# A two-layer block with test-time training, experts and latent attention: attention's weight folds cut into pieces behind single heads, their transposes made by loads and VectorE, and the values' bias as weighted sums

## The chip, the cores and the metric

The kernel runs on one core of a Trainium2 chip. The metric is the device time of one execution in microseconds. TensorE is called PE below, VectorE DVE, ScalarE ACT, GpSimd POOL; SP (SyncE) issues most of the transfers.

## The reference

The model is two residual blocks in float32 over x of shape [4, 512, 512]. Block one adds a test-time-training attention (a scan of 32 mini-batches of 16 tokens, which updates a small weight matrix per head in each step) and a gated feed-forward of width 1408. Block two adds a latent attention (16 heads of 128 over 512 tokens, as four sequences) and four experts, where token t goes to expert t mod 4. The change concerns block two's attention and the last lines of block one:

```python
c_kv = hidden_states @ W_DKV + b_DKV
k = (c_kv @ W_UK + b_UK).reshape(b, s, H, D)
v = (c_kv @ W_UV + b_UV).reshape(b, s, H, D)
c_q = hidden_states @ W_DQ + b_DQ
q = (c_q @ W_UQ + b_UQ).reshape(b, s, H, D)
...
q_r = q @ W_QR
k_r = k @ W_KR
...
q = q.at[..., :RD].set(rope(q_r))
k = k.at[..., :RD].set(rope(k_r))
scores = jnp.einsum('bqhd,bkhd->bhqk', q, k) / jnp.sqrt(jnp.float32(D))
probs = jax.nn.softmax(scores, axis=-1)
ctx = jnp.einsum('bhqk,bkhd->bqhd', probs, v).reshape(b, s, H * D)
return ctx @ W_O + b_O
```

H is 16, D 128, RD 64. c_kv has 128 columns and c_q 384 (three tiles of 128).

## The kernel before, in words

**Folded weights.** The kernel multiplies weights with weights so as to save work per token. Per head, W_UK W_KR and W_UQ W_QR (128 to 64 columns) take the place of the rotated half of keys and queries, and W_UV W_O (128x512, called vo) lets the latents themselves be the values. Each product contracts over D, so the weight must be turned first. `group_weights(hg)` does that for a group of four heads: it loads uk, uq0 to uq2, uv and W_O's rows ow (L948, L962); five times it turns a block's four 128x128 squares on PE against the identity (ptw, L937) and copies the result out of PSUM with ACT (wt, L939); four of the blocks are multiplied by W_KR or W_QR (pw, L955; copied by ACT, L956), the fifth by ow, four times (pvo, L970; copied, L971). The values' bias b_UV becomes a constant row through W_O, since a softmax row sums to 1: b_O + W_O^T b_UV, the tile bo. `value_bias(hg)` computes it during the first stage: 16 loads of W_O rows (wob), 16 matmuls with b_UV spread over 32 columns, and for each group a matmul with ones (1/32) and an add.

**Stage 1, the scan** (0 to about 946 us). The 32 steps run in sequence; 4 steps are a chunk, 8 chunks (NCHUNK) the whole. Between the parts of a step stands other PE work, the filler: next chunk's keys and queries, feed-forward tiles, the norm and output projection of finished chunks (`finish`), `value_bias`, and the second block's latents. This order is written out by hand: every generator yields the PE time of its piece in microseconds, and `fill(us)` takes pieces until that much is used. START, three GAPS per step, LAST_GAPS for the last chunk and LAST_FINISH for the pieces of the last `finish` set how much. A scheduler then orders each engine's queue.

**The tail of stage 1** (946 to 1022 us): the last chunk's z goes through DRAM to zb, is normed twice and projected (L546 to L601). `latents(key)` multiplies the normed rows by W_DKV and W_DQ; each of four 128-column results m is copied out by ACT with its bias, one quarter per sequence (L637), into a tile lat of two buffers and stored to DRAM (lat_d, L640, on ACT's queue). POOL's queue meanwhile loads the experts' gate weights and the rows xe (14 of 16; the last two on SP, L831).

**Stage 2, the experts** (1022 to 1191 us): for each of four experts, four pairs of gate and up products (epg, epu, L855), SiLU on ACT, a product on DVE (inter), then four down products (epo, L900), added to y by DVE (L907), and y += bo by POOL (L908). All PSUM tiles come from one pool d_ps.

**Stage 3, attention** (1191 to 2161 us): 64 units (4 groups of heads, 4 sequences, 4 heads). Per unit: keys and queries (pk L992, pq L999) with the rotation by DVE (L978, L982) and an add on POOL (L985); scores (sc L1008), row maximum (mx L1010, DVE), exponentials and their scaling (L1013, L1015, ACT); DVE turns 32x32 blocks (tt, L1023); 16 transfers per unit, all on SP, put the blocks in place (prT<-tt, L1046); three units later the context (pc L1054), and per four units the output projection (po L1069). `group_weights` of the next group stands ahead of the unit where sequence 1 begins; group 0's ahead of the first unit.

Of the kernel before, what the change touches and what calls it, by code (L numbers as in the profile page):

```python
# [12 lines left out]
F32 = mybir.dt.float32  # L13
AF = mybir.ActivationFunctionType
# [21 lines left out]
START = 20.0  # L36
GAPS, LAST_GAPS = (11.0, 4.0, 8.0), (10.0, 4.0, 5.0)
LAST_FINISH = (9.0, 17.0, 5.0)
TTT_EPS = 1e-6
# [16 lines left out]
def trunk_kernel(ctx: ExitStack, tc: tile.TileContext, a: dict, out: bass.AP):  # L56
# [32 lines left out]
    with ExitStack() as px:  # L89
# [423 lines left out]


        ones32 = one.tile([P, P], F32, tag="ones32", name="ones32")
        nc.vector.memset(ones32, 1.0 / 32)
        buv16 = one.tile([H, D], F32, tag="buv16", name="buv16")
        nc.gpsimd.dma_start(out=buv16, in_=a["b_UV"].rearrange("(h d) -> h d", d=D))
        buv_b = one.tile([P, H, 32], F32, tag="buv_b", name="buv_b")
        nc.gpsimd.dma_start(out=bo, in_=a["b_O"].unsqueeze(0).to_broadcast([P, HS]))  # L520

        def value_bias(hg):
            if hg == 0:
                pt = psum()[:, :H]
                nc.tensor.transpose(pt, buv16, ident[:H, :H])
                nc.vector.tensor_copy(buv_b, pt.unsqueeze(2).to_broadcast([P, H, 32]))
            pb = psum()
            for h, r in enumerate(quarters):
                w = wk.tile([P, HS], F32, tag="wd", name=f"wob_{hg}_{h}", bufs=4)
                nc.sync.dma_start(out=w, in_=a["W_O"][(4 * hg + h) * D : (4 * hg + h + 1) * D, :])  # L530
                mm(pb[r], buv_b[:, 4 * hg + h, :], w)
            part = wk.tile([P, HS], F32, tag="xt", name=f"bo_part{hg}", bufs=4)
            nc.vector.tensor_copy(part, pb)
            yield 1.3
            pb = psum()
            mm(pb, ones32, part)
            nc.vector.tensor_add(bo, pb, bo)
            yield 0.86

        def over_blocks(t, z):  # L540
# [83 lines left out]
        def latents(key):  # L624
# [4 lines left out]
            for m, w in enumerate(lw):  # L629
                pl = psum()[:, : n * CW]  # L630
                for c in range(NC):
                    mm(pl, w[:, c, :], part[:, :, c], c == 0, c == NC - 1)
                st = wk.tile([P, 512], F32, tag="xs", name=f"lat_{ks[0]}_{m}")
                view = pl.rearrange("p (k u e b j) -> p k u e b j", k=n, u=2, e=E, b=2)
                to = st[:, : n * CW].rearrange("p (b k e j) -> p b k e j", b=B, k=n, e=E)
                for b in range(B):
                    nc.scalar.activation(  # L637
                        to[:, b], view[:, :, b // 2, :, b % 2], AF.Identity, bias=lat_b[:, m : m + 1], scale=1.0
                    )
# [6 lines left out]
        nc.gpsimd.dma_start(out=lat_b[:, :1], in_=a["b_DKV"])  # L646
        nc.gpsimd.dma_start(out=lat_b[:, 1:], in_=a["b_DQ"])


        def between(ch):  # L650
# [10 lines left out]
            if ch == 0:  # L661
                yield from finish_constants()
            extra = value_bias(ch - 1) if 1 <= ch <= NHG else iter(())
            nxt = iter(())
# [12 lines left out]
            yield from extra  # L677
            yield from nxt
# [116 lines left out]
        for us in LAST_FINISH:  # L795
            fill(us)
            next(fin)
        for _ in chain(work, fin, latents(NCHUNK - 1)):
            pass
# [19 lines left out]
    lv = lat.tile([P, B, E, KVC], F32, tag="lv", name="lv")  # L819

    with ExitStack() as px:
        one = px.enter_context(tc.tile_pool(name="d_one", bufs=1, reuse_waits="tile"))
        wk = px.enter_context(tc.tile_pool(name="d_wk", bufs=2, reuse_waits="tile"))
        wg = px.enter_context(tc.tile_pool(name="d_wg", bufs=1, reuse_waits="tile"))
        psp = px.enter_context(tc.tile_pool(name="d_ps", bufs=2, space=PSUM))
        gate_w = [one.tile([P, NC, 2 * EI], F32, tag="gu1", name="gu_1")]
        gate_w.insert(0, wg.tile([P, NC, 2 * EI], F32, tag="gu0", name="gu_0"))
# [41 lines left out]
        for e in range(E):  # L869
# [3 lines left out]
            if e == 1:  # L873
                nc.sync.dma_start(out=wqr, in_=a["W_QR"])
                nc.sync.dma_start(out=wkr, in_=a["W_KR"])
                nc.sync.dma_start(out=buk, in_=a["b_UK"])
                nc.sync.dma_start(out=buq, in_=a["b_UQ"])
# [9 lines left out]
            for i in range(EI // P):  # L887
                pg = psp.tile([P, B * P], F32, tag="pg", name=f"epg_{e}_{i}")
                product(e, pg, gu, i * P)
                pu = psp.tile([P, B * P], F32, tag="pu", name=f"epu_{e}_{i}")  # L890
                product(e, pu, gu, EI + i * P)
# [5 lines left out]
            for b in range(B):  # L897
# [9 lines left out]
                nc.vector.tensor_add(y[b][:, e, :], po, y[b][:, e, :])  # L907
                nc.gpsimd.tensor_add(y[b][:, e, :], y[b][:, e, :], bo)  # L908
            if e == 1:

                for wr, bias in ((wkr, buk), (wqr, buq)):
                    pb = psp.tile([P, 512], F32, tag="pa", name="pb")
                    nc.tensor.matmul(pb[RD:, :H], lhsT=wr, rhs=bias, start=True, stop=True)
                    nc.vector.tensor_copy(bias[RD:, :], pb[RD:, :H])
                nc.vector.tensor_scalar_mul(buq[:RD, :], buq[:RD, :], scale)
                nc.vector.tensor_scalar_mul(trig_q[RD:, :], trig_k[RD:, :], scale)
# [11 lines left out]
    with ExitStack() as px:  # L928
        wk = px.enter_context(tc.tile_pool(name="e_wk", bufs=2, reuse_waits="tile"))
        ps_pj = px.enter_context(tc.tile_pool(name="e_pspj", bufs=4, space=PSUM))  # L930
        ps_sc = px.enter_context(tc.tile_pool(name="e_pssc", bufs=4, space=PSUM))

        def turned(w, nm):

            pt = ps_pj.tile([P, HPG, P], F32, tag="pj", name=f"ptw_{nm}")
            for h in range(HPG):
                nc.tensor.transpose(pt[:, h, :], w[:, h, :], ident)  # L937
            t = wk.tile([P, HPG, P], F32, tag="wt", name=f"wt_{nm}")
            nc.scalar.copy(t, pt)  # L939
            return t  # L940

        def group_weights(hg):

            c = slice(hg * HPG * D, (hg + 1) * HPG * D)

            def loaded(name, src, bufs=2):
                t = wk.tile([P, HPG, src.shape[-1] // HPG], F32, tag=name, name=f"{name}_{hg}", bufs=bufs)
                nc.sync.dma_start(out=t, in_=src.rearrange("p (h d) -> p h d", h=HPG))  # L948
                return t

            def fold(w, wr, nm):
                wt = turned(w, f"{nm}_{hg}")
                pw = ps_pj.tile([P, HPG, RD], F32, tag="pj", name=f"pw_{nm}_{hg}")
                for h in range(HPG):
                    nc.tensor.matmul(pw[:, h, :], lhsT=wt[:, h, :], rhs=wr, start=True, stop=True)  # L955
                nc.scalar.copy(w[:, :, RD:], pw)  # L956

            uk = loaded("uk", a["W_UK"][:, c])
            uq = [loaded(f"uq{i}", a["W_UQ"][i * P : (i + 1) * P, c]) for i in range(QC // P)]
            uv = loaded("uv", a["W_UV"][:, c], bufs=1)  # L960
            ow = wk.tile([P, HPG, HS], F32, tag="ow", name=f"ow_{hg}", bufs=1)
            nc.sync.dma_start(out=ow, in_=a["W_O"][c, :].rearrange("(h p) o -> p h o", p=P))  # L962
            fold(uk, wkr, "uk")
            for i in range(QC // P):
                fold(uq[i], wqr, f"uq{i}")
            uvt = turned(uv, f"uv_{hg}")
            vo = wk.tile([P, HPG, HS], F32, tag="vo", name=f"vo_{hg}")
            for h in range(HPG):
                pv = ps_pj.tile([P, HS], F32, tag="pj", name=f"pvo_{hg}_{h}")
                nc.tensor.matmul(pv, lhsT=uvt[:, h, :], rhs=ow[:, h, :], start=True, stop=True)  # L970
                nc.scalar.copy(vo[:, h, :], pv)  # L971
            return dict(uk=uk, uq=uq, vo=vo)

# [13 lines left out]
        def queries_keys(hg, b, h, w):  # L987
# [10 lines left out]
            for i in range(nq):  # L998
                nc.tensor.matmul(  # L999
                    pq, lhsT=w["uq"][i][:, h, :], rhs=cq[:, i, b, :], start=(i == 0), stop=(i == nq - 1)  # L1000
                )
# [208 lines left out]
```

## Time and profile before

| | us |
|---|---|
| three runs, median | 2162.95 |
| three runs, lowest and highest | 2159.44, 2164.58 |
| the profiled execution | 2162.4 |
| its span in the trace | 2160.6 |
| mean granted PE clock | 0.987 |

The profile's page gives the busy time of each engine, the span in 40 equal slices, the transfers, the chain of work that ended last, and the costliest groups of instructions. These are its slices for PE and its clock, in tenths, and for the transfers' rate:

```profile
PE   8999999999999999995999899999999999999998
...
PEclk9999999999999999998999989999999999999999
DMA  6556364646474646526610233333233333333332
GB/s 179 153 138 190 112 193 134 180 135 175 131 197 129 173 136 192 171 75 235 226 59 25 89 92 77 74 94 75 76 77 93 75 72 78 75 75 75 95 94 76
```

One digit covers 54 us; a 9 stands for 90% or more. The 5 is the tail of stage 1. By groups, in PE, the largest of stage 3 and the transfers that belong to it:

```profile
L1008 PE MATMUL sc<-kT,qT 96*128 96x512 f32 x512 | 235.7, 598 | 15.1 <-ACT prob L1013 13.5
...
L1023 DVE STREAM_TRANSPOSE tt<-prob 128x512 f32<-128x512 f32 x252 | 166.6, 697 | 60.3 <-ACT prob L1015 56.7
...
prT<-tt SPq DMA_DIRECT2D x1008, 64.0 KB, 2.0
```

A group's row gives line, engine, operation, output and inputs, the shape and the number of instructions; then busy time and the mean of one in ns; then the idle time of the engine just before, and what ended most of it. The last row gives KB of one transfer and the median time from issue to landing. A matmul of float32 shows as two records.

### The profile page before, as it was taken

The numbers are of one execution on the slowest core, as the hardware profiler recorded it, in microseconds if no ns is written. First come the engines' busy times: TensorE is split into PE (matmuls) and PEld (weight loads), VectorE is DVE, ScalarE is ACT, GpSimd is POOL, SyncE is SP. The second block draws the span as 40 slices with busy tenths as digits, with TensorE's granted clock in tenths as the row PEclk, the third lists the DMA queues.
The fourth block names the chain that finished last, engine by engine and source line by source line (L and its number), as shares of the span: only waits on it lengthen the run. The fifth ranks groups of instructions, "written<-read, shape, count | busy, mean of one in ns | idle before, by whom it ended". The sixth has DMA issues, their size and how long they took to land.

```text
span 2160.6 us, 29279 instructions
## 1 busy us (share of the span) xinstructions
PE 2068.6 (96%) x10050; PEld 1181.5 (55%) x10050; DVE 1177.5 (54%) x2384; ACT 883.3 (41%) x1805; POOL 504.9 (23%) x555
## 2 busy tenths in 40 slices
PE   8999999999999999995999899999999999999998
PEld 6776676767676767543444444444444444444444
DVE  4445656465656565631111556664666656666663
ACT  2334353434434343332000454444544545455552
POOL 4233233233333333301001211110111111111110
PEclk9999999999999999998999989999999999999999
DMA  6556364646474646526610233333233333333332
GB/s 179 153 138 190 112 193 134 180 135 175 131 197 129 173 136 192 171 75 235 226 59 25 89 92 77 74 94 75 76 77 93 75 72 78 75 75 75 95 94 76
DMA packets 286960, 259.27 MB, mean 120 GB/s; under 512 B 52956, under 2 KB 210845, under 8 KB 285789
## 3 DMA queue, kind: packets, MB, share of 16 engines
q1 hardware_dynamic: 272752, 245.96, 41.0%
q10 hardware_dynamic: 11500, 5.32, 0.9%
q0 software_dynamic: 2560, 6.13, 0.8%
q8 instruction: 81, 1.33, 0.3%
q14 instruction: 67, 0.54, 0.1%
HBM read 161.60 MB, written 29.62 MB: 89 GB/s over the span
## 4 chain that ended last, share of the span: by engine, by line
PE 75%; DVE 10%; ACT 9%; DMA 3%; issue 2%; POOL 1%; SPq 0%; ACTq 0%; DVEq 0%; POOLq 0%
PE pj L100 14%; PE pf L100 11%; PE po L1069 10%; PE pc L1054 7%; PE sc L1008 5%; PE pq L999 5%; PE pd L100 5%; ACT prob L1013 3%; PE epg L855 3%; PE epo L900 3%; PE epu L855 3%; ACT prob L1015 2%; PE pso L100 2%; PE pk L992 2%; PE pz L100 2%
## 5 line engine op out<-in xcount | busy, mean ns | idle before, releaser
L1008 PE MATMUL sc<-kT,qT 96*128 96x512 f32 x512 | 235.7, 598 | 15.1 <-ACT prob L1013 13.5
L985 POOL TENSOR_TENSOR kT<-t_k,t_k 32x512 f32<-32x512 f32 x64 | 80.7, 1261 | 717.9 <-PE pq L999 403.3
L1013 ACT ACTIVATE prob<-sc,mx 128x512 f32<-128x512 f32 x256 | 173.1, 683 | 147.1 <-DVE mx L1010 147.1
L1069 PE MATMUL po<-vo,ctxT 128*128 128x512 f32 x512 | 223.0, 593 | 1.5 <-ACT ctxT L1059 1.5
L1054 PE MATMUL pc<-prT,lv 128*128 128x512 f32 x496 | 224.0, 594 | 0.0
L1023 DVE STREAM_TRANSPOSE tt<-prob 128x512 f32<-128x512 f32 x252 | 166.6, 697 | 60.3 <-ACT prob L1015 56.7
L100 PE MATMUL pf<-xT,wg 128*128 128x256 f32 x704 | 171.8, 385 | 4.2 <-DVE hid L459 3.9
L999 PE MATMUL pq<-cq,uq 128*128 128x512 f32 x384 | 175.2, 592 | 0.0
L1015 ACT ACTIVATE prob<-prob,sm 128x512 f32<-128x512 f32 x256 | 171.7, 724 | 3.6 <-DVE sm L1014 3.6
L1008 PEld LDWEIGHTS sc<-kT,qT 96*128 96x128 f32 x512 | 96.0, 191 | 140.9 <-issue 110.6
L100 PE MATMUL pf<-xT,wu 128*128 128x256 f32 x704 | 168.0, 380 | 0.5 <-DMA wu<-in_wu 0.3
L1010 DVE TENSOR_REDUCE mx<-sc 128x1 f32<-128x512 f32 x256 | 164.4, 681 | 7.0 <-PE sc L1008 4.4
L100 PE MATMUL pd<-wd,hid 128*128 128x512 f32 x352 | 165.2, 600 | 0.2
L1069 PEld LDWEIGHTS po<-vo,ctxT 128*128 128x128 f32 x512 | 97.1, 190 | 124.1 <-issue 116.2
L1054 PEld LDWEIGHTS pc<-prT,lv 128*128 128x128 f32 x496 | 94.5, 191 | 120.0 <-issue 112.1
L100 PEld LDWEIGHTS pf<-xT,wg 128*128 128x128 f32 x704 | 131.0, 190 | 32.1 <-DVE hid L459 6.7
L100 PEld LDWEIGHTS pf<-xT,wu 128*128 128x128 f32 x704 | 133.2, 190 | 22.1 <-issue 2.6
L1079 DVE TENSOR_TENSOR y<-po,y 128x512 f32<-128x512 f32 x64 | 44.2, 691 | 152.5 <-PE po L1069 152.5
L993 ACT ACTIVATE kT<-pk,b_UK 64x512 f32<-64x512 f32 x64 | 43.7, 683 | 196.7 <-PE pk L992 196.7
L999 PEld LDWEIGHTS pq<-cq,uq 128*128 128x128 f32 x384 | 73.0, 190 | 91.8 <-issue 86.8
L459 DVE SCALAR_TENSOR_TENSOR hid<-pf,us,sg 128x256 f32<-128x256 f32 x88 | 41.5, 474 | 132.6 <-ACT sg L458 132.0
L297 POOL TENSOR_SCALAR sk<-k,m 128x256 f32<-128x256 f32 x64 | 61.3, 969 | 158.1 <-PE pz L100 158.1
(256 smaller groups left out, 3151.8 us busy)
## 6 DMA issues: line engine op xcount, KB each, us to landing
prT<-tt SPq DMA_DIRECT2D x1008, 64.0 KB, 2.0
wd<-in_wd SPq DMA_DIRECT2D x176, 256.0 KB, 3.0
wg<-in_wg SPq DMA_DIRECT2D x88, 256.0 KB, 3.5
wu<-in_wu SPq DMA_DIRECT2D x88, 256.0 KB, 3.4
rows<-rows SPq DMA_DIRECT2D x128, 66.0 KB, 2.2
kv<-rows SPq DMA_DIRECT2D x32, 264.0 KB, 4.4
gu<-in_gu SPq DMA_DIRECT2D x3, 2048.0 KB, 8.7
xt<-in_x SPq DMA_DIRECT2D x32, 128.0 KB, 3.2
```

Of the source, the lines that this page charges most:

```text
L100: nc.tensor.matmul(out, lhsT=lhsT, rhs=rhs, start=start, stop=stop, skip_group_check=True)
L855: nc.tensor.matmul(ps, lhsT=w[:, c, col : col + P], rhs=xe[:, :, c, e, :], start=(c == 0), stop=(c == NC - 1))
L900: nc.tensor.matmul(po, lhsT=inter[:, i, b * P : (b + 1) * P], rhs=dn[:, i, :], start=(i == 0), stop=(i == EI // P - 1),)
L985: nc.gpsimd.tensor_sub(t[RD:mid, :], t1[RD:mid, :], t2[RD:mid, :])
L999: nc.tensor.matmul(pq, lhsT=w["uq"][i][:, h, :], rhs=cq[:, i, b, :], start=(i == 0), stop=(i == nq - 1))
L1008: nc.tensor.matmul(ps, lhsT=qT[:KQ, i * P : (i + 1) * P], rhs=kT[:KQ, :], start=True, stop=True)
L1010: nc.vector.tensor_reduce(mx, ps, AX.X, ALU.max, negate=True)
L1013: nc.scalar.activation(pr, ps, AF.Exp, bias=mx, scale=1.0, accum_out=sm)
L1015: nc.scalar.mul(pr, pr, sm)
L1023: nc.vector.transpose(out=tt[:, :, :, i, :], in_=pr.rearrange("p (kb e j) -> p kb e j", e=2, j=K))
L1054: ins = nc.tensor.matmul(pc, lhsT=lv[:, b, k, :], rhs=prT[:, k, :], start=(k == 0), stop=(k == E - 1))
L1069: ins = nc.tensor.matmul(po[e], lhsT=ctxT[:, h, e * P : (e + 1) * P], rhs=w["vo"][:, h, :], start=(h == 0), stop=(h == HPG - 1),)
```

## The change

Its parts:

- The filler's budgets: the middle gap of a step is 3 for 4, in the last chunk (10, 3, 7) for (10, 4, 5); LAST_FINISH has six entries, and after them come the last latents, then the rest of the filler.
- `value_bias` is gone from stage 1. Each fold multiplies its heads' ow rows by b_UV (one scalar per row) on DVE into a running sum bo_part; after the last group one matmul with ones sums over rows and adds to bo. POOL's y += bo goes from the experts to the last 16 units of attention.
- `latents`: odd m are copied out by DVE, even m by ACT.
- In the experts, gate and up tiles have a PSUM pool of their own, ps_gu.
- `fold` takes the place of `group_weights`. For uk and uq only the RD columns that stay are loaded into the weight tile. The block to be turned comes as 16 loads of 32 partitions with four runs of 128 bytes each (raw), which put the 32x32 squares where the transpose wants them; DVE's stream transpose turns the squares (wt). ow is loaded by heads. `fold` yields between pieces: block i is loaded, block i-1 turned, block i-2 multiplied.
- Group 0's fold runs in pieces among experts 1 to 3, with one buffer each for raw and wt; the others' advance by a piece behind each unit whose head isn't the first of a sequence, with two buffers each.

```diff
-GAPS, LAST_GAPS = (11.0, 4.0, 8.0), (10.0, 4.0, 5.0)
-LAST_FINISH = (9.0, 17.0, 5.0)
+GAPS, LAST_GAPS = (11.0, 3.0, 8.0), (10.0, 3.0, 7.0)
+LAST_FINISH = (10.0, 14.0, 7.0, 0.0, 3.0, 1.0)
...
-        def value_bias(hg):
...
-            for h, r in enumerate(quarters):
-                w = wk.tile([P, HS], F32, tag="wd", name=f"wob_{hg}_{h}", bufs=4)
-                nc.sync.dma_start(out=w, in_=a["W_O"][(4 * hg + h) * D : (4 * hg + h + 1) * D, :])
-                mm(pb[r], buv_b[:, 4 * hg + h, :], w)
...
                 for b in range(B):
...
+                    part_b = view[:, :, b // 2, :, b % 2]
+                    if m % 2:
+                        nc.vector.tensor_scalar(to[:, b], part_b, lat_b[:, m : m + 1], None, ALU.add)
+                    else:
+                        nc.scalar.activation(to[:, b], part_b, AF.Identity, bias=lat_b[:, m : m + 1], scale=1.0)
...
-        for _ in chain(work, fin, latents(NCHUNK - 1)):
+        for _ in chain(latents(NCHUNK - 1), work):
             pass
...
+    def fold(w, hg, wk, psum, bufs):
...
+        for nm, src in zip(ups, srcs):
+            nc.sync.dma_start(out=w[nm][:, :, :RD], in_=src.rearrange("p (h d) -> p h d", h=HPG)[:, :, :RD])
...
+        def output_rows(h):
+            ows[h] = wk.tile([P, HS], F32, tag="ow", name=f"ow_{hg}_{h}", bufs=2)
+            nc.sync.dma_start(out=ows[h], in_=a["W_O"][(hg * HPG + h) * D : (hg * HPG + h + 1) * D, :])
...
+        for i in range(n + 2):
+            if 0 <= i - 2 < n - 1:
+                wt, wr, to = turned.pop(i - 2), wkr if i == 2 else wqr, w[ups[i - 2]]
+                pw = psum(f"pw_{hg}_{i}").rearrange("p (h d) -> p h d", h=HPG)[:, :, :RD]
+                for h in range(HPG):
+                    nc.tensor.matmul(pw[:, h, :], lhsT=wt[:, h, :], rhs=wr, start=True, stop=True)
+                nc.scalar.copy(to[:, :, RD:], pw)
+            if 0 <= i - 1 < n:
+                t = turned[i - 1] = wk.tile([P, HPG, P], F32, tag="wt", name=f"wt_{hg}_{i - 1}", bufs=bufs)
+                nc.vector.transpose(
+                    out=t.rearrange("p h c -> p (h c)"), in_=raws.pop(i - 1).rearrange("p h c -> p (h c)")
+                )
+            if i < n:
+
+                raw = raws[i] = wk.tile([P, HPG, P], F32, tag="raw", name=f"raw_{hg}_{i}", bufs=bufs)
+                view = srcs[i].rearrange("(cq r) (h dq d) -> dq r h cq d", r=32, h=HPG, dq=4)
+                for dq, r in enumerate(quarters):
+                    for h in range(HPG):
+                        nc.sync.dma_start(
+                            out=raw[r, h].rearrange("r (cq d) -> r cq d", cq=4), in_=view[dq, :, h]
+                        )
+            if i >= n:
+                output_rows(i - n)
+            yield
+        wt = turned.pop(n - 1)
+        for h in range(HPG):
+            pv = psum(f"pvo_{hg}_{h}")
+            nc.tensor.matmul(pv, lhsT=wt[:, h, :], rhs=ows[h], start=True, stop=True)
+            nc.scalar.copy(w["vo"][:, h, :], pv)
+            hh = hg * HPG + h
+            if hh == 0:
+                nc.vector.tensor_scalar_mul(bo_part, ows[h], buv[:, :1])
+            else:
+                nc.vector.scalar_tensor_tensor(bo_part, ows[h], buv[:, hh : hh + 1], bo_part, ALU.mult, ALU.add)
+            if h + 2 < HPG:
+                output_rows(h + 2)
+            if h == 1:
+                yield
+        if hg == NHG - 1:
+            pb = psum("pbo")
+            nc.tensor.matmul(pb, lhsT=ones, rhs=bo_part, start=True, stop=True)
+            nc.vector.tensor_add(bo, pb, bo)
...
+        ps_gu = px.enter_context(tc.tile_pool(name="d_psgu", bufs=2, space=PSUM))
...
+                first = fold(w0, 0, wk, lambda nm: psp.tile([P, 512], F32, tag="pa", name=nm), 1)
...
             for i in range(EI // P):
-                pg = psp.tile([P, B * P], F32, tag="pg", name=f"epg_{e}_{i}")
+                if e > 1:
+                    next(first, None)
+                pg = ps_gu.tile([P, B * P], F32, tag="pg", name=f"epg_{e}_{i}")
...
-                nc.gpsimd.tensor_add(y[b][:, e, :], y[b][:, e, :], bo)
+            if e in (1, 2):
+                next(first, None)
...
-        ws[0] = group_weights(0)
+        folds = iter(())
+        ws[0] = w0
...
-                        ws[hg + 1] = group_weights(hg + 1)
+                        ws[hg + 1] = group_tiles((lat, wk)[(hg + 1) % 2], hg + 1)
+                        folds = fold(
+                            ws[hg + 1], hg + 1, wk, lambda nm: ps_pj.tile([P, 512], F32, tag="pj", name=nm), 2
+                        )
...
+            if i % HPG != 0:
+                next(folds, None)
+            if 0 <= i - len(units) + HPG * B < HPG * B:
+                b, e = divmod(i - len(units) + HPG * B, HPG)
+                nc.gpsimd.tensor_add(y[b][:, e, :], y[b][:, e, :], bo)
```

More of the change, by code (lines that the diff above doesn't have):

```diff
@@ L512, in finish_constants @@
             yield 3.43
[L515 to L520, printed above, removed]
-        def value_bias(hg):
[L523 to L527, printed above, removed]
-            for h, r in enumerate(quarters):
-                w = wk.tile([P, HS], F32, tag="wd", name=f"wob_{hg}_{h}", bufs=4)
-                nc.sync.dma_start(out=w, in_=a["W_O"][(4 * hg + h) * D : (4 * hg + h + 1) * D, :])
-                mm(pb[r], buv_b[:, 4 * hg + h, :], w)
[L532 to L538, printed above, removed]
         def over_blocks(t, z):
@@ L636, in latents @@
                 for b in range(B):
-                    nc.scalar.activation(
-                        to[:, b], view[:, :, b // 2, :, b % 2], AF.Identity, bias=lat_b[:, m : m + 1], scale=1.0
-                    )
+                    part_b = view[:, :, b // 2, :, b % 2]
[3 more added lines that the diff above has]
+                        nc.scalar.activation(to[:, b], part_b, AF.Identity, bias=lat_b[:, m : m + 1], scale=1.0)
                 nc.scalar.dma_start(
@@ L646, in trunk_kernel @@
         nc.gpsimd.dma_start(out=lat_b[:, :1], in_=a["b_DKV"])
+        nc.gpsimd.dma_start(out=bo, in_=a["b_O"].unsqueeze(0).to_broadcast([P, HS]))
         nc.gpsimd.dma_start(out=lat_b[:, 1:], in_=a["b_DQ"])
@@ L662, in between @@
                 yield from finish_constants()
-            extra = value_bias(ch - 1) if 1 <= ch <= NHG else iter(())
             nxt = iter(())
@@ L676, in between @@
                     yield from take(fin, 1)
-            yield from extra
             yield from nxt
@@ L819, in trunk_kernel, with group_tiles @@
     lv = lat.tile([P, B, E, KVC], F32, tag="lv", name="lv")
+    quarters = [slice(32 * q, 32 * q + 32) for q in range(4)]
+    buv = lat.tile([P, H], F32, tag="b_UV", name="b_UV")
+    bo_part = lat.tile([P, HS], F32, tag="bo_part", name="bo_part")
+    ones = lat.tile([P, P], F32, tag="ones", name="ones")
+    nc.gpsimd.memset(ones, 1.0)
+    ups = ["uk"] + [f"uq{i}" for i in range(QC // P)]
+    def group_tiles(pool, hg):
+        w = {nm: pool.tile([P, HPG, D], F32, tag=nm, name=f"{nm}_{hg}", bufs=1) for nm in ups}
+        w["vo"] = pool.tile([P, HPG, HS], F32, tag="vo", name=f"vo_{hg}", bufs=1)
+        return w
@@ new lines, in fold @@
+    def fold(w, hg, wk, psum, bufs):
+        c = slice(hg * HPG * D, (hg + 1) * HPG * D)
+        srcs = [a["W_UK"][:, c]] + [a["W_UQ"][i * P : (i + 1) * P, c] for i in range(QC // P)]
+        for nm, src in zip(ups, srcs):
+            nc.sync.dma_start(out=w[nm][:, :, :RD], in_=src.rearrange("p (h d) -> p h d", h=HPG)[:, :, :RD])
+        srcs.append(a["W_UV"][:, c])
+        raws, turned, ows = {}, {}, {}
+        def output_rows(h):
+            ows[h] = wk.tile([P, HS], F32, tag="ow", name=f"ow_{hg}_{h}", bufs=2)
+            nc.sync.dma_start(out=ows[h], in_=a["W_O"][(hg * HPG + h) * D : (hg * HPG + h + 1) * D, :])
+        n = len(srcs)
+        for i in range(n + 2):
[39 more added lines that the diff above has]
+            nc.vector.tensor_add(bo, pb, bo)
@@ L875, in trunk_kernel @@
                 nc.sync.dma_start(out=wkr, in_=a["W_KR"])
+                buv16 = wk.tile([H, D], F32, tag="buv16", name="buv16", bufs=1)
+                nc.sync.dma_start(out=buv16, in_=a["b_UV"].rearrange("(h d) -> h d", d=D))
+                w0 = group_tiles(lat, 0)
+                first = fold(w0, 0, wk, lambda nm: psp.tile([P, 512], F32, tag="pa", name=nm), 1)
                 nc.sync.dma_start(out=buk, in_=a["b_UK"])
@@ L887, in trunk_kernel @@
             for i in range(EI // P):
-                pg = psp.tile([P, B * P], F32, tag="pg", name=f"epg_{e}_{i}")
+                if e > 1:
+                    next(first, None)
+                pg = ps_gu.tile([P, B * P], F32, tag="pg", name=f"epg_{e}_{i}")
                 product(e, pg, gu, i * P)
-                pu = psp.tile([P, B * P], F32, tag="pu", name=f"epu_{e}_{i}")
+                pu = ps_gu.tile([P, B * P], F32, tag="pu", name=f"epu_{e}_{i}")
                 product(e, pu, gu, EI + i * P)
@@ L914, in trunk_kernel @@
                     nc.vector.tensor_copy(bias[RD:, :], pb[RD:, :H])
+                pb = psp.tile([P, 512], F32, tag="pa", name="pbuv")
+                nc.tensor.transpose(pb[:, :H], buv16, ident[:H, :H])
+                nc.vector.tensor_copy(buv, pb[:, :H])
                 nc.vector.tensor_scalar_mul(buq[:RD, :], buq[:RD, :], scale)
@@ L931, in trunk_kernel @@
         ps_sc = px.enter_context(tc.tile_pool(name="e_pssc", bufs=4, space=PSUM))
[L933 to L972, printed above, removed]
         def rotate(t, ps, bias, trig, nm):
@@ L999, in queries_keys @@
                 nc.tensor.matmul(
-                    pq, lhsT=w["uq"][i][:, h, :], rhs=cq[:, i, b, :], start=(i == 0), stop=(i == nq - 1)
+                    pq, lhsT=w[f"uq{i}"][:, h, :], rhs=cq[:, i, b, :], start=(i == 0), stop=(i == nq - 1)
                 )
```

## The prediction

> **What bounds the kernel now.** I read the page first: busy time by engine, then the chain of work that ended last.
>
> ```profile
> PE 2068.6 (96%) x10050; PEld 1181.5 (55%) x10050; DVE 1177.5 (54%) x2384; ACT 883.3 (41%) x1805; POOL 504.9 (23%) x555
> ...
> PE 75%; DVE 10%; ACT 9%; DMA 3%; issue 2%; POOL 1%; SPq 0%; ACTq 0%; DVEq 0%; POOLq 0%
> ```
>
> TensorE is the bound: only 92 us of the 2160.6 us span are idle on it. So a gain is either a matmul taken away or one of these idle stretches closed. Next, windows by stage show where they lie. In the scan:
>
> ```profile
> 54.00:400.00 346.00, 334.06 (x2609) 241.76 (x2608) 190.39 (x443) 138.14 (x250) 106.89 (x134) 0.99 0.53 151
> 400.00:900.00 500.00, 488.81 (x3925) 355.82 (x3924) 299.22 (x668) 204.83 (x376) 170.95 (x205) 1.00 0.57 164
> ```
>
> The second number is the window's length, the third PE busy: 97 to 98%, so PE work removed here is time removed. Between scan and experts it is otherwise:
>
> ```profile
> 963.13:981.26 18.13, 16.46 (x52) 9.66 (x53) 9.21 (x6) 8.27 (x26) 5.92 (x8) 1.00 0.25 70
> 981.26:993.57 12.31, 0.60 (x3) 0.22 (x2) 2.34 (x3) 1.98 (x5) 4.68 (x9) 0.69 1.04 404
> 993.57:1008.48 14.91, 11.57 (x28) 5.62 (x29) 4.84 (x11) 2.02 (x5) 0.00 (x0) 0.80 0.34 102
> 1008.48:1022.40 13.92, 7.18 (x33) 6.00 (x33) 0.00 (x0) 3.71 (x16) 0.00 (x0) 0.91 0.82 255
> ```
>
> From the scan's end at 946.25 to the first expert matmul at 1022.40 are 76.15 us with 49.81 busy: 26.3 idle, at a clock down to 0.69. The timelines of PE and ACT tell what ends the waits:
>
> ```profile
> 993.57 0.98 PE L100 MATMUL pj<-onesd,pn_sq 128*128 128x1 f32 x4 [11.71 <-DVE pn_sq L543]
> ...
> 1022.40 2.07 PE L855 MATMUL epg<-xe,gu 128*128 128x512 f32 x2 [6.74 <-ACT lat L637]
> ```
> ```profile
> 989.66 0.93 ACT L637 ACTIVATE lat<-pj,lat_b 128x64 f32<-128x64 f32 x4 [8.70 <-DMA lat_d<-lat]
> ...
> 1019.84 0.93 ACT L637 ACTIVATE lat<-pj,lat_b 128x64 f32<-128x64 f32 x4 [6.67 <-DMA lat_d<-lat]
> ```
>
> A bracket is the idle time before the row and its releaser. Twice ACT stands 7 to 9 us for the store of a latent tile two tiles back, under loads of 404 GB/s. The first hold keeps up the last chunk's norm, the second the first expert matmul, which waits for PSUM that ACT frees. The experts (1022.4 to 1191.3) are all PE: 168.90 busy of 168.90. Then the first fold stands alone:
>
> ```profile
> 1192.75 0.63 PE L937 MATMUL ptw_uk<-ident,uk 128*128 128x128 f32 x4 [0.83 <-issue]
> ...
> 1204.43 5.31 PE L970 MATMUL pvo<-ow,wt_uv 128*128 128x512 f32 x8 [0.73 <-ACT wt_uv L939]
> 1209.58 0.59 PE L992 MATMUL pk<-ckv,uk 128*128 128x512 f32 x1
> ```
>
> Three rows price the rest:
>
> ```profile
> L100 PE MATMUL pj<-wob,buv_b x32: 592/593/1057, 262.5 to 611.0; 128*32 128x512 f32 x32
> L277 SPq DMA_DIRECT2D rows<-rows x128: 303/430/1938, 31.2 to 827.5; - x128
> L1046 SPq DMA_DIRECT2D prT<-tt x1008: 585/599/1982, 1227.7 to 2137.0; - x168
> ```
>
> **The change, part by part** (against the profiled execution: 2162.4 us, span 2160.6; the median of the runs, 2162.95, is 0.5 above).
>
> 1. *value_bias out of the scan.* 16 wob matmuls of two records; a pair steps by about 0.98 us, so 15.7; four ones matmuls at 0.86 (a pair like pk's, 1.02 with its overlap), 3.4; one transpose 0.15. **−19**: PE has 2 to 3% idle there, so it all counts, unless the gaps' smaller fill (middle gap 4 to 3) uncovers the scan's serial chain; then −10. Its replacement, 16 DVE weighted sums of 0.75 us, lies among experts and attention, where the windows show DVE 14 and 62 to 67% busy: nothing; uncovered 12.
>
> 2. *Tail.* With pg and pu in PSUM of their own, the first expert matmul waits for DMAs only: the 6.7 us go, and about 2 us of half-clock records behind them. Half the latent evacuations go to DVE and one chunk's latents (13.7 us of PE work) are left for the end: they fill idle time. But ACT's and DVE's order of the changed kernel still has latent tiles, each waiting for a store two tiles back, between the steps of the last norm, and xe's last two stores behind them on ACT. So I don't credit the 8.7 us hold; it may move to another step of the norm. Ends: −2 (a new hold eats it) and −24 (nearly all idle gone). Taken: 6.7 + 2 + 3 of filled idle: **−12**.
>
> 3. *Group 0's fold among the experts.* Added to a stage with no idle PE: four pw of 0.84 (1491.80 to the next start at 1492.64 in group 2), four pvo matmuls in 3.5, pbuv 0.15: +7. wt_3 on DVE stands ahead of inter_3 and waits for 16 raw loads: behind it epo's operand and PE; bounded by 0 and one burst (7), taken +1; the cold fold start goes, −2. **+6**. The 18.1 us from 1191.3 to pk at 1209.4 go: **−18**. What is late next is pk's operands cq and ckv, loaded by then in both.
>
> 4. *Folds 1 to 3.* 15 blocks of four PE transposes at 0.44 (start to next start, 1489.63 to 1490.08), 6.6 us. The waits for wt copies are 0.7 + 8.4 + 2.8 = 11.9 in all groups (waits by releaser), less 3.6 in group 0: 8.3. Now wt comes from DVE a unit (10 us) before PE wants it. **−15**. DVE gets 20 stream transposes of 0.70 (tt's row): hidden; each waits for 16 loads, with mx and tt queued behind, and sc and prT behind those; a burst plus landing is 6.9 + 2, under the 10 us of a unit.
>
> 5. *320 raw loads on SP*, the unknown. SP issues 16 prT per unit, 10.3 us of a PE unit of 10.3 (13.7 with po); the order has 48 of a group's 80 raw loads between units 22 and 26 (likewise 6 to 10, 38 to 42). From the first prT of 22 (1567.5) to the last that 26's context (1637.7) allows are 58 us with landing; four units' prT take 41. So the stall per group is 48c − 17, where c is the issue of one raw load. Ends: 0.30 (the rows' minimum) gives none, with 1 at unit 23, whose slack is 4.6; 0.60 (prT) gives 12; 0.43 gives 4. A raw load reads DRAM in 128 runs, as rows' loads move 128 runs; prT goes SBUF to SBUF. I take 0.43: 3 × 4 = **+12**, with +3 and +36 as ends. The 12 further ow loads (about 0.4 each, 5 us) follow unit 26, where SP stands idle for DVE's tt (239 us in all); uk and uq stay four issues per group.
>
> Here the Trainium skill speaks against the change: "DMA: Bandwidth & Descriptors", Bandwidth, says transfers under 64 KB are descriptor-dominated and lists 0.68 us of engine time for 4 KB, 0.95 for 64 KB. A raw load is 16 KB in 128 B runs; interpolated between these, an estimate of 0.75 us each would make the stall 19 per group, 57 in all, and the whole time 2165: no gain. In this trace prT, itself 64 KB, lands after 2.0 us yet one is issued each 0.6: three or more are under way at once. So I take the issue, not the transfer.
>
> 6. *y += bo on POOL in the last 16 units*, 1.26 each. Nine stand back to back before group 3's first kT and qT: 11 us that rotations wait behind, and sc behind them; one to two units of lead cover most. With pbo 0.9: **+3** (1 to 12).
>
> Sum: −19 − 12 + 6 − 18 − 15 + 12 + 3 = −43; 2162.4 − 43 = 2119.4, with the 0.5 of the median **2120**.
>
> **Rivals.**
>
> - *Raw loads at prT's 0.60*: part 5 becomes 36, 2144 (2135 to 2158). For it: the same 32 partitions and four runs on each; against: rows and kv at 0.43. 18%.
> - *Slower: SP becomes the bound in the attention.* The other parts sum to −55; they are eaten from 48c − 17 = 18.4 on, c = 0.74. At c = 1.0, as trig's four strided loads show in the median (1.02, lanes waited for), 31 per group, 93 in all: 2201. SP's queue is in order, so prT, the contexts and DVE's tt all stand behind a burst. Against: trig's loads meet the 2 MB expert loads. 9%.
> - *Scan and tail give nothing back*: gaps too short (−10) and the latents hold the last norm (−2): +19, 2139. For it: ACT's order; against: the PSUM wait goes in any case. 12%.
> - *More than forecast*: raw loads at 0.30 (+3) and the tail −24: 2099. 13%.
>
> My forecast (2106 to 2135) has 48%. The range holds forecast, cheap and dear raw loads and the lost tail: **2092 to 2154**. A measurement can't tell under 0.2% (4.3 us) from no change. Faster 0.88, same 0.03, slower 0.09.
>
> **What would show it.** SP's row for raw: 0.43, and prT of units 7, 10, 23, 26, 39, 42 waiting on nothing but the queue, with pc there idle 2 to 5 us. Experts about 176 us long, their first matmul without ACT as releaser, within 70 us of the scan's end. No gap after the last epo. Scan 19 us shorter. In all, PE busy falls by about 27 us (19, and 9 of 80 transposes, less pbuv and pbo) and its idle by about 16. I am wrong if raw issues take 0.6 or more, if DVE waits for raw loads while sc waits for mx, or if ACT still stands on latent stores during the last norm.

## The result: slower by 2.7%, and the profile after

| | us |
|---|---|
| before, median of 4 runs | 2163.76 |
| the changed kernel, median of 4 runs | 2222.43 (2216.11 to 2222.76) |
| ratio, 95% interval | 1.0267 (1.0243 to 1.0291) |
| its profiled execution: span | 2220.5 |

The forecast was 2120. On the page of the changed kernel, TensorE is busy for longer than before although it executes 118 instructions less, and the scores' row has another releaser:

```profile
PE 2074.2 (93%) x9932; PEld 1177.6 (53%) x9932; DVE 1204.0 (54%) x2452; ACT 851.6 (38%) x1733; POOL 505.2 (23%) x555
...
L1025 PE MATMUL sc<-kT,qT 96*128 96x512 f32 x512 | 261.5, 652 | 55.2 <-POOL qT L1002 37.4
```

Before, this group took 235.7 us at 598 ns each, behind 15.1 us of idle time. A mean of 652 ns means that part of the scores ran slower; the timelines below show them at half clock. Windows by stage say where the time is. First before, from the scan to the end; then the changed kernel, cut at the same events (last matmul of the scan, first epg, first pk). The third number is PE busy; the granted clock stands behind POOL's busy time:

```profile
0.00:946.30 946.30, 913.98 (x7197) 655.80 (x7197) 540.92 (x1240) 370.98 (x699) 312.78 (x395) 0.99 0.55 157
946.30:1022.40 76.10, 49.76 (x150) 27.45 (x147) 16.98 (x22) 22.18 (x72) 10.60 (x16) 0.89 0.56 178
1022.40:1209.60 187.20, 182.79 (x465) 84.62 (x466) 23.89 (x36) 19.15 (x33) 20.22 (x16) 0.97 0.31 110
1209.60:2160.60 951.00, 922.08 (x2245) 413.59 (x2243) 595.70 (x1086) 470.94 (x1003) 161.25 (x128) 0.99 0.32 81
```
```profile
0.00:928.40 928.40, 888.33 (x7124) 647.48 (x7124) 538.57 (x1233) 350.68 (x668) 313.41 (x394) 0.99 0.54 154
928.40:1035.50 107.10, 65.22 (x179) 33.99 (x178) 25.94 (x61) 16.79 (x49) 10.75 (x17) 0.82 0.54 180
1035.50:1214.00 178.50, 177.60 (x446) 80.96 (x446) 29.47 (x46) 16.92 (x29) 0.00 (x0) 0.98 0.31 90
1214.00:2220.50 1006.50, 943.06 (x2186) 415.17 (x2186) 610.02 (x1114) 467.25 (x987) 181.00 (x144) 0.96 0.33 78
```

Scan −17.9, tail +31.0, experts with the first fold −8.7, attention +55.5: together +59.9, the difference of the spans. The scan gained about what was forecast (−19), and the experts with the first fold a part of it (+6 − 18 = −12); the tail and the attention went the other way. In the attention PE has 59 instructions less and 21 us more busy time, and 63 us of idle time where it had 29. The list of PE's waits (total, times, longest) has the largest of each at its head:

```profile
PE sc L1025 <- POOL qT L1002: 37.4, 12, 5.9
PE epg L903 <- DMA xe<-xe_d: 33.6, 1, 33.6
```

**The tail.** The first expert matmul no longer waits for ACT, as forecast; it waits for the rows xe. POOL's timeline shows why they are late:

```profile
964.34 0.83 POOL L892 DMA_DIRECT2D gu<-in_gu  x1
1005.79 4.26 POOL L896 DMA_DIRECT2D xe<-xe_d  x8 [40.62 <-DMA lat_d<-lat]
```

The gate weights go out behind POOL's last addition, as before; the next instruction, xe's first load, stands 40.6 us and is released by a store of latents. Nothing in the diff connects these two. The addresses in the built programs do (bytes in each partition):

```
xe before: 167232 to 200000, over kv, sk, km, wh, xh, grad and others of the scan
xe after:  194944 to 227712, over wd, zb, pn_sq, pn_rs and, from 221728, the latents' two tiles (lat)
```

The new weights of group 0, bo_part and the fold's tiles are allocated ahead of xe, which moves up by 27,712 bytes: from tiles that are dead when the scan ends onto those that the last norm and the latents use to the very end.

**The attention.** PE's timeline around unit 5 (the second unit whose scores follow the first four):

```profile
1268.94 1.02 PE L1009 MATMUL pk<-ckv,uk 128*128 128x512 f32 x2
1269.79 2.74 PE L1016 MATMUL pq<-cq,uq 128*128 128x512 f32 x6
1272.37 1.02 PE L1025 MATMUL sc<-kT,qT 96*128 96x512 f32 x2
1276.41 5.48 PE L1025 MATMUL sc<-kT,qT 96*128 96x512 f32 x6 [3.02 <-POOL qT L1002]
1281.69 4.39 PE L1071 MATMUL pc<-prT,lv 128*128 128x512 f32 x8
```

Keys and queries, the last score of the unit before, and then at once this unit's own scores. From pq to sc lies ACT's bias, two DVE products and POOL's addition, 4 to 6 us in all (in unit 30 pq ends at 1667.0 and sc starts at 1672.8). Nothing else stands in PE's queue to cover it; PE waits 3 us, and the six records behind take 5.48 us, where eight take 3.60 elsewhere: half clock (the granted clock from 1276.41 to 1281.69 is 0.50). The unit takes 17 us, not 10.3. Before, in the same unit, the scores behind pq are those of unit 4, and a context and the next unit's keys and queries stand ahead of its own:

```profile
1273.91 1.02 PE L992 MATMUL pk<-ckv,uk 128*128 128x512 f32 x2
1274.77 2.74 PE L999 MATMUL pq<-cq,uq 128*128 128x512 f32 x6
1277.35 3.60 PE L1008 MATMUL sc<-kT,qT 96*128 96x512 f32 x8
1280.78 3.60 PE L1054 MATMUL pc<-prT,lv 128*128 128x512 f32 x8
```

The lead of the scores can be read from PE's order alone, by summing the matmuls between a unit's last pq and its first sc:

```
unit          4     5     6    13    14    26    29    30
before      6.9  10.3  24.1  10.3   3.4   3.4  10.3   3.4   us
changed     1.7   0.9   0.9   1.7   0.0   1.7   3.4   0.0
```

Units 42, 45 and 46 are as 26, 29 and 30. These are the places of the long waits for qT, but for one at unit 49 (e6).

### The profile page after: what moved, and what is told of

Read it like the earlier page. It is cut to its first block, busy times and chain, and to the rows that moved or that the text cites. A ratio compares the mean times of both kernels' runs of the same rounds, so it can differ in the third digit from the quotient of the medians.

```text
span 2220.5 us, 29394 instructions
## 1 busy us (share of the span) xinstructions
PE 2074.2 (93%) x9932; PEld 1177.6 (53%) x9932; DVE 1204.0 (54%) x2452; ACT 851.6 (38%) x1733; POOL 505.2 (23%) x555
## 4 chain that ended last, share of the span: by engine, by line
PE 38%; ACT 7%; DVE 5%; issue 1%; POOL 1%; DMA 1%; SPq 1%; DVEq 0%; POOLq 0%; ACTq 0%
PE po L1086 10%; PE pc L1071 6%; PE sc L1025 6%; PE pq L1016 5%; ACT prob L1030 3%; PE epg L903 3%; PE epo L954 2%; PE epu L903 2%; ACT prob L1032 2%; PE pk L1009 2%; DVE t_q L995 1%; DVE t_q L999 1%; DVE mx L1027 1%; SPq L1063 1%; DVE t_k L999 1%
## 5 line engine op out<-in xcount | busy, mean ns | idle before, releaser
L1025 PE MATMUL sc<-kT,qT 96*128 96x512 f32 x512 | 261.5, 652 | 55.2 <-POOL qT L1002 37.4
L1071 PE MATMUL pc<-prT,lv 128*128 128x512 f32 x496 | 229.5, 606 | 0.0
L1025 PEld LDWEIGHTS sc<-kT,qT 96*128 96x128 f32 x512 | 102.5, 205 | 198.5 <-issue 115.0
L459 DVE SCALAR_TENSOR_TENSOR hid<-pf,us,sg 128x256 f32<-128x256 f32 x88 | 41.9, 478 | 141.1 <-ACT sg L458 140.4
```

The source lines that it names most:

```text
L1025: nc.tensor.matmul(ps, lhsT=qT[:KQ, i * P : (i + 1) * P], rhs=kT[:KQ, :], start=True, stop=True)
L1071: ins = nc.tensor.matmul(pc, lhsT=lv[:, b, k, :], rhs=prT[:, k, :], start=(k == 0), stop=(k == E - 1))
```

## The experiments

Theory A: xe's place in SBUF and the order of the scores, two things that no line of the diff states, cost the time. Theory B: the transfers do, SP's queue in the attention and the load on the DMA engines in the tail.

**e1_xe_low: xe elsewhere.**

```diff
+        dnp = px.enter_context(tc.tile_pool(name="d_dn", bufs=2, reuse_waits="tile"))
+        wg = px.enter_context(tc.tile_pool(name="d_wg", bufs=1, reuse_waits="tile"))
         wk = px.enter_context(tc.tile_pool(name="d_wk", bufs=2, reuse_waits="tile"))
-        wg = px.enter_context(tc.tile_pool(name="d_wg", bufs=1, reuse_waits="tile"))
...
-            dn = wk.tile([P, EI // P, HS], F32, tag="dn", name=f"dn_{e}")
+            dn = dnp.tile([P, EI // P, HS], F32, tag="dn", name=f"dn_{e}")
```

> Only the places in SBUF differ from the changed kernel: the two dn buffers are allocated ahead of gu0 and xe, the rest of that pool behind them, so that xe lies on the scan's own buffers and no longer on those of the last norm and of the latents. Theory A (the first expert matmul is late because xe's loads wait for memory that the last latent stores still read): xe's loads go out behind POOL's add at about 964 us, the 33.6 us wait at the experts' start falls to under 8, and the whole time is about 2190 (2222 less 33). Theory B (the loads are late because the transfers of gu, y and dn fill the DMA engines, wherever xe lies): the wait stays above 20 us and the time above 2210. The attention is as in the changed kernel, about 1006 us from the first pk.

Measured: 2197.61 (ratio to before 1.0168, 1.0146 to 1.0191). xe's first load goes out at 965.4 us, right behind the gate weights, and the wait for xe is gone:

```profile
1007.88 3.60 PE L904 MATMUL epg<-xe,gu 128*128 128x512 f32 x8
```

The tail takes 78.2 us instead of 107.1. Theory A holds for the tail. The total fell by 25, not 33: with the experts starting earlier, the next wait shows among them (7.4 us of epu for inter; below, e5).

**e2_order: scores behind the next unit's queries.** The issue order alone; all loads stay where they are.

```diff
...
-                nc.tensor.matmul(
+                pqs[hg, b, h] = nc.tensor.matmul(
...
-                probs[i - 1] = turn(softmax(*qk.pop(i - 1), f"{i - 1}"), f"{i - 1}")
+                with ExitStack() as pinned:
+                    if i >= 2:
+                        pinned.enter_context(tc.issue_after(pqs[units[i]].ins))
+                    tt_u = softmax(*qk.pop(i - 1), f"{i - 1}")
+                probs[i - 1] = turn(tt_u, f"{i - 1}")
```

> Only TensorE's order in the attention differs from the changed kernel: the scores of a unit are held behind the last pq matmul of the next unit, an issue order alone. All 240 raw loads of groups 1 to 3 stay on SP in their places. Theory A (the attention lost its time because scores stand right behind their own keys and queries in units 4 to 6, 13, 14, 26, 29, 30, 42, 45 and 46, so that the chain through ACT, DVE and POOL is bare): the 37.4 us of sc waiting for POOL's qT fall to under 8, the half-clock matmuls behind them go too, the attention takes 955 to 965 us in place of 1006, the whole about 2175. Theory B (SP's queue, filled with raw loads, is the limit): prT is late all the same, pc waits for it, and the time stays above 2205.

Measured: 2156.34 (0.9972, 0.9958 to 0.9987). The attention falls from 1006.5 to 941.7 us, and sc waits 5.8 us for qT. The attention's window, and PE's timeline at the same units:

```profile
1211.20:2152.90 941.70, 917.17 (x2186) 407.34 (x2186) 612.49 (x1114) 462.23 (x987) 181.42 (x144) 0.99 0.36 84
```
```profile
1258.27 1.02 PE L1011 MATMUL pk<-ckv,uk 128*128 128x512 f32 x2
1259.13 2.74 PE L1018 MATMUL pq<-cq,uq 128*128 128x512 f32 x6
1261.71 3.60 PE L1027 MATMUL sc<-kT,qT 96*128 96x512 f32 x8
1265.14 3.60 PE L1073 MATMUL pc<-prT,lv 128*128 128x512 f32 x8
```

Without a bracket, at full clock, 10.3 us from pk to pk. With the same instructions PE's busy time in the attention is 917.2 us, 25.9 less than in the changed kernel: so much did the half clock behind the short waits cost, beside 39 us of idle time. SP's queue was not the main thing.

**e3_both: both edits.**

> Both edits, xe's place and the order of the scores. If both causes are right and apart, the gains add: about 2142 (2222 less 33 less 47), which is faster than the kernel before (2163) by 1%. If they overlap or raise another wait, it is above 2160.

Measured: 2136.66 (0.9885, 0.9862 to 0.9908); together they give 86 of the 91 us that the two gave alone (25 and 66). This is faster than before, with every part of the change in it.

**e4_both_raw_act: and the raw loads off SP.**

```diff
-                        nc.sync.dma_start(
+                        (nc.scalar if hg else nc.sync).dma_start(
                             out=raw[r, h].rearrange("r (cq d) -> r cq d", cq=4), in_=view[dq, :, h]
                         )
```

> As e3_both, but the raw loads of groups 1 to 3 are issued by ACT's queue in place of SP's, 240 issues of about 0.43 us moved, 34 us per group. If SP's queue still costs time once the order is held (the 4 us per group of the prediction), this is 8 to 12 us faster than e3_both. If it does not, the two are within 4 us, or this one slower by what ACT's exponentials lose to the issues (up to 10).

Measured: 2124.94 (0.9838, 0.9813 to 0.9864), 11.7 us less. So theory B has its share: with the order held, SP's queue still cost 12 us. It falls in groups 2 and 3: from unit 26's pk to 27's 30.8 us become 24.9, from 42's to 43's 29.4 become 25.0. The row that shows it in e2_order is unit 23's context, one of two late places where pc waits (the other is unit 39's, 2.38 us):

```profile
1564.95 6.71 PE L1073 MATMUL pc<-prT,lv 128*128 128x512 f32 x8 [2.61 <-ACT prob L1032]
```

The bracket names ACT's prob, but a wait for several things is put down to the one that the profile has last. SP's timeline tells which it was: it issues 13 raw loads from 1546.20 to 1552.73, and unit 23's 16 prT only behind them, from 1552.84. At 0.6 us each and 2.0 us to landing they are in place at about 1564.4. With the loads on ACT's queue the wait is gone.

**e5_trig_later: a DVE product behind its load.** In e3_both, DVE's timeline among the first expert's products, and PE's at the same time:

```profile
1013.75 0.69 DVE L949 TENSOR_TENSOR inter<-epu,esg 128x512 f32<-128x512 f32 x1 [4.67 <-issue]
1037.78 0.42 DVE L975 TENSOR_SCALAR trig_q<-trig_k 64x512 f32<-64x512 f32 x1 [23.34 <-DMA trig_k<-in_trig]
```
```profile
1038.98 6.48 PE L904 MATMUL epu<-xe,gu 128*128 128x512 f32 x8 [8.16 <-DVE inter L949]
```

trig_q isn't wanted before the attention, but stands in DVE's order behind inter_0, waits for a load, and inter_1 with it, until PE has no PSUM tile left. (Before, DVE waited there too, 11.0 us, but PE was busy throughout the experts.) The edit, on top of e4_both_raw_act, holds it behind the third expert.

```diff
-                nc.vector.tensor_scalar_mul(trig_q[RD:, :], trig_k[RD:, :], scale)
             if e == 2:
+                tc.keep_in_program_order(nc.vector.tensor_scalar_mul(trig_q[RD:, :], trig_k[RD:, :], scale))
```

> As e4_both_raw_act, and DVE's multiplication trig_q is held behind the third expert's additions; in e3_both and e4_both_raw_act it stood between inter_0 and inter_1 of the first expert and waited 23 us for trig_k's load, and PE's epu waited 7 to 8 us behind it. Theory: the experts take 177 us in place of 184, the whole about 2117. If the wait only passes to another row, under 3 us are gained.

Measured: 2116.07 (0.9791, 0.9766 to 0.9816); experts and first fold 175.7 us where e4_both_raw_act took 184.9.

**e6_adds_in_order: POOL's additions one by one.** In the changed kernel POOL's timeline at the start of group 3 is:

```profile
1958.03 7.39 POOL L1129 TENSOR_TENSOR y<-y,bo 128x512 f32<-128x512 f32 x6 [4.74 <-issue]
1965.50 1.26 POOL L1002 TENSOR_TENSOR kT<-t_k,t_k 32x512 f32<-32x512 f32 x1
1966.84 6.15 POOL L1129 TENSOR_TENSOR y<-y,bo 128x512 f32<-128x512 f32 x5
1973.07 1.25 POOL L1002 TENSOR_TENSOR qT<-t_q,t_q 32x512 f32<-32x512 f32 x1
```

Eleven additions around one kT, and its qT behind them. The edit, on top of e5_trig_later, holds each in its place.

```diff
-                nc.gpsimd.tensor_add(y[b][:, e, :], y[b][:, e, :], bo)
+                tc.keep_in_program_order(nc.gpsimd.tensor_add(y[b][:, e, :], y[b][:, e, :], bo))
```

> As e5_trig_later, and POOL's 16 additions y += bo keep the program's order, one behind each unit's qT, so that no run of them stands ahead of group 3's first qT. Theory: the 7 us by which unit 49 starts late (17.6 us from pk to pk where 10.3 is the rule) go, the whole 6 to 7 us less than e5_trig_later, about 2111. If the additions are covered in any case: within 2 us of e5_trig_later.

Measured: 2108.39 (0.9751, 0.9729 to 0.9772), 7.7 us less; the two intervals just meet, but the traces agree: unit 49 takes 10.3 us, where it took 17.4.

**e7_before_order: a control.** The same holding of the scores in the kernel before.

> The kernel before with the scores' order held in the same way, and nothing else: what the order is worth without the change. Its scores already stand 3.4 to 24 us behind their queries, so that theory A expects little, 0 to 18 us (sc waits 13.5 us for ACT in all, and steady stretches of 13 units took 4 us less in e2_order): 2145 to 2163. If it gains 40 us or more, most of what e2_order gained had nothing to do with the change.

Measured: 2172.43 (1.0050, 1.0034 to 1.0066): slower, outside what was expected. Steady batches of four units did win 0.7 us each, but each fold, all in one place there, takes 7 to 9 us more from unit 19 to 20 and 35 to 36 (32.2 and 34.0 us, where 25.4 were), with most of its matmuls at half clock. So the hold is no gain by itself; what it gave in e2_order belongs to the order of the changed kernel.

**e8_one_load: what made the order short.** In groups 1 to 3 one load brings each block, and its squares are not put in their places; nothing holds the order.

```diff
+                if hg:
+                    nc.sync.dma_start(out=raw, in_=srcs[i].rearrange("p (h d) -> p h d", h=HPG))
-                for dq, r in enumerate(quarters):
+                for dq, r in enumerate(quarters if hg == 0 else []):
```

> The changed kernel, but for groups 1 to 3 each block comes by one load in place of 16, so that the 32x32 squares stay where they are and these groups' folded weights are other numbers; SP issues 225 loads less. Nothing holds the order. In the order as built the lead of the scores is whole again in units 26, 29, 30, 42, 45 and 46 (3.4 to 24.9 us where it was 0 to 3.4) and as short as ever in units 4 to 6. Theory (raw loads on SP make the scheduler put scores late queries first, the missing fold of group 1 makes units 4 to 6 short): groups 2 and 3 win 10 to 14 us each, group 1 10 or so, units 4 to 6 stay at 17 us apiece; the whole 2222 less 30 to 40, about 2187. If the order had nothing to do with the raw loads, the whole falls by at most the 12 us that SP's queue was worth.

Measured: 2168.95 (1.0032, 1.0021 to 1.0044). From group to group (unit 15 to 31, 31 to 47) 228.9 us twice, where the changed kernel takes 249.2 twice; unit 0 to 15 takes 218.0 in place of 233.5. Units 4 and 5 remain at 16.4 and 16.6. So the raw loads cost about 20 us per group. In the same two stretches e2_order returned 14 and 16 us by the order alone, and e4_both_raw_act 8 and 6 more by SP's queue: most of the cost is the order that the scheduler chose with the loads in the queue. That order is a decision at build time, not something that the chip does. The gain, 53, was larger than expected (30 to 40); how much of group 1's 15 us is which wasn't told apart.

Units 4 to 6 have another cause, since they are as slow without the raw loads. It is argued from the timelines and was not tested: the kernel before had group 1's fold there, 20 us of PE work between unit 3 and 4, under which ACT and DVE caught up with the first four units. Taking it away left the start uncovered: unit 8 starts 109.0 us behind unit 0 before, 111.2 in the changed kernel, and 92.9 with the order held (e2).

**e9_psum_shared and e12_lat_act: two parts of the tail undone**, from e6_adds_in_order: the experts' PSUM pool, and DVE's half of the latents.

```diff
-                pg = ps_gu.tile([P, B * P], F32, tag="pg", name=f"epg_{e}_{i}")
+                pg = psp.tile([P, B * P], F32, tag="pg", name=f"epg_{e}_{i}")
...
-                pu = ps_gu.tile([P, B * P], F32, tag="pu", name=f"epu_{e}_{i}")
+                pu = psp.tile([P, B * P], F32, tag="pu", name=f"epu_{e}_{i}")
```

> As e6_adds_in_order, with ps_gu undone: the experts' gate and up tiles come from d_ps again, so that the first epg waits for the last latents to leave PSUM (ACT and DVE) as well as for the loads. The prediction put 6.7 us and 2 us of half clock on this part. With xe's loads early and half the latents on DVE the last of them is out about 3 us behind their matmuls: 2 to 4 us slower than e6_adds_in_order if that is all, 7 to 9 if the part is worth what was predicted, and equal if the last loads of xe end later anyway.

Measured: 2110.35 (0.9765, 0.9744 to 0.9786). PE stands 3.0 us ahead of the first epg.

```diff
-                    if m % 2:
-                        nc.vector.tensor_scalar(to[:, b], part_b, lat_b[:, m : m + 1], None, ALU.add)
-                    else:
+                    if True:
                         nc.scalar.activation(to[:, b], part_b, AF.Identity, bias=lat_b[:, m : m + 1], scale=1.0)
```

> As e6_adds_in_order, but all latents are copied out of PSUM by ACT, as before the change. If DVE's half matters, ACT's queue holds the last norm longer and the first experts' SiLU: 3 to 8 us slower. If DVE's copies only brought another hold on DVE (4.3 us of PE waiting for them in e6_adds_in_order), it is equal or up to 4 us faster.

Measured: 2109.82 (0.9761, 0.9740 to 0.9781). Both intervals overlap that of e6_adds_in_order: neither part is shown to be worth anything by itself here, with xe early and the other edits in place. For the PSUM pool the trace has the 3.0 us and not the 8.7 of the prediction.

**e10_lat_four: four buffers for the latents**, from e6_adds_in_order. What still holds the tail in e3_both, on ACT and, one step on, PE:

```profile
982.29 0.93 ACT L615 ACTIVATE lat<-pj,lat_b 128x64 f32<-128x64 f32 x4 [11.61 <-DMA lat_d<-lat]
```
```profile
983.27 8.77 PE L100 MATMUL pj<-wo,zb 128*128 128x512 f32 x16 [3.92 <-ACT lat L615]
```
```diff
-                st = wk.tile([P, 512], F32, tag="xs", name=f"lat_{ks[0]}_{m}")
+                st = wk.tile([P, 512], F32, tag="wd", name=f"lat_{ks[0]}_{m}", bufs=4)
```

> As e6_adds_in_order, and the latents' tiles on their way to DRAM have four buffers (those of the down weights, which are free by then) in place of two. Theory: what still holds the tail is a latent copy that stands in ACT's or DVE's order ahead of a step of the last norm and waits for the store two tiles back (11.6 us on ACT and 5.6 on DVE in e3_both, of which PE waited 8.2 us); with four the waits go, the tail takes about 69 us in place of 77.5, the whole about 2100. Rival: the stores are slow under the loads of gu and xe whatever their number, and the wait stays: within 2 us of e6_adds_in_order.

Measured: 2098.30 (0.9703, 0.9686 to 0.9719), 3.0% faster than before, the best version; it holds the edits of e1 to e6 as well. Its windows of tail and attention:

```profile
928.20:996.40 68.20, 61.62 (x181) 33.12 (x179) 25.13 (x57) 16.73 (x49) 10.77 (x17) 0.97 0.57 177
...
1172.10:2095.70 923.60, 910.79 (x2186) 406.28 (x2186) 613.24 (x1114) 467.46 (x987) 183.24 (x144) 0.99 0.36 86
```

The tail has 6.6 us of idle time left of the 41.9 of the changed kernel, the attention 12.8 of 63.4.

**e11_pe_turn: PE's transposes again, but in pieces**, from e6_adds_in_order.

```diff
+                if hg:
+                    pt, raw = psum(f"ptw_{hg}_{i}"), raws.pop(i - 1)
+                    for h in range(HPG):
+                        nc.tensor.transpose(pt[:, h * P : (h + 1) * P], raw[:, h, :], ident)
+                    nc.scalar.copy(t.rearrange("p h c -> p (h c)"), pt)
```

> As e6_adds_in_order, but in groups 1 to 3 each block comes by one load and its four squares are turned by TensorE and copied by ACT, as before the change, in the same pieces behind the units. It adds 60 transposes of 0.11 us, 6.6 us of PE work, and 15 ACT copies of 0.6 us; it takes 240 load issues from ACT and 15 stream transposes from DVE. If TensorE alone decides: 6 to 7 us slower, about 2115. If ACT's issues cost something too, it is nearer to equal, 0 to 4 us slower.

Measured: 2116.04 (0.9788, 0.9774 to 0.9803), 7.7 us more than e6_adds_in_order. The load-and-DVE transposes are worth about the 6.6 us of PE work that they save, once the loads aren't in prT's queue.

## Why the prediction was wrong, step by step

1. *value_bias, −19*: close in time, −17.9, but by luck. Not only value_bias left the scan (its groups took 17.4 us of PE) but also a chunk of latents (14.4 us), 32 us in all. PE busy fell by 25.7 us and its idle time rose by 8. "It all counts" did not hold for what was taken away, and what the latents would free in the scan was put at nothing. Smaller gaps may be the reason for the idle time, which wasn't tried.
2. *Tail, −12*: wrong in sign, +31. The step that failed is "with pg and pu in PSUM of their own, the first expert matmul waits for DMAs only: the 6.7 us go". It does wait for loads only, but the loads weren't followed back one instruction further: xe's first load waits for whatever lies under it, and the change moves it. e1 shows 29 us of it in the trace. A second term failed with it: without that wait (e1) the tail is still 2 us longer than before. Idle time there falls by 12, as forecast, from 26.3 us to 14.6; but the latents that left the scan are 13.7 us of work here, and the sum had them as filling idle time only. The 8.7 us hold, which wasn't credited, came back on the last norm (e3), as one of the prediction's own signs of being wrong had it, and was worth about 10 (e10).
3. *Group 0's fold, +6 − 18*: measured +8.1 (experts 177.6 for 169.5) and −16.8. Right.
4. *Folds 1 to 3, −15*: the transposes' own saving of 6.6 is right (e11); the 8.3 us of waits were not measured apart. But the step looked only at the fold and not at what was late next, the scores of units 4 to 6, which seem to have lost their cover; holding the order gains 18 us there (111.2 to 92.9 from unit 0 to 8).
5. *Raw loads, +12*: the price was right, 430 ns in the median:

```profile
L843 SPq DMA_DIRECT2D raw<-in_W_UQ x192: 311/430/1922, 1080.3 to 1868.4; - x192
```

   So was the stall that follows from it: 11.7 us by e4, where the estimate of 0.75 us each, from the transfer times of the Trainium skill ("DMA: Bandwidth & Descriptors", Bandwidth, measured there on GpSimd's queue), made it 57. With the order held (e2), pc stood idle 2.6 and 2.4 us at units 23 and 39, two of the places that were named; group 1 shows no such wait. The step that failed is the order, a term that the sum does not have: the loads in SP's queue changed where the scheduler puts the scores, and that cost 30 us in groups 2 and 3 (e2) and an untold part of group 1's. The lead of the scores was taken as before's, without reading it off the changed order.
6. *POOL's additions, +3*: mis-sized, 7.7 (e6), though within its stated 1 to 12. "One to two units of lead cover most" assumed a lead; what counts is that the whole run stands ahead of one qT.

The rival on the slow side (SP the bound from 0.74 us per load) gave the right sign for another reason: the loads took 0.43. With both hidden costs gone (e3) the kernel comes to 2137 and without POOL's, trig_q's and SP's shares (e6) to 2108. That the forecast of 2120 lies between is luck too, after the terms above.

## What to carry to other kernels

A diff doesn't state two things that this change altered: where later tiles lie, and in which order a scheduler issues what it doesn't touch. Before costing the parts, compare in the built program which waits the first load of the next stage has, and sum the work between each producer and its consumer on the bounding engine; a lead that falls below the chain through the other engines is a stall, and here it could be read without a run. Work that moves from one stage to another stands in the sums of both. And ask of every stretch of work that is taken off the bound what was catching up beneath it.

## What the runs showed of the hardware

- Short waits cost twice. Ten of the 12 waits for qT took 2 to 6 us; with all but one of them gone (e2), PE was busy 26 us less for the same instructions. After the wait of 3.02 us at 1276.41 the granted clock was 0.50 for the next 5 us; after one of 1.38 us at 1236.79 it stayed at 1.00.
- Loads of 16 KB in runs of 128 bytes from DRAM were issued at one per 0.43 us in the median on SP, and about as fast on ACT's queue (0.44), landing 1.8 us after issue. No run shows a cost of their size or short runs beyond the issue.
